# A two-layer graph kernel: the late tiles' exp moved from ScalarE to a power on GpSimd while the second layer's slots run

## Chip, cores, metric

The kernel runs on one core of a Trainium2 chip. The metric is the device time of one execution in microseconds, lower is better. Times below are the median of several runs and one profiled execution with its trace.

## What is computed

Two layers follow each other on 2708 rows of 256 values. Each is an attention over a 0/1 adjacency matrix and then a mixture of eight experts, of which every row takes two. Cut to what matters here, the second layer's expert part is:

```
xf     = layernorm(x)                            # [2708, 256]
probs  = softmax(xf @ gate_w + gate_b)           # [2708, 8]
top2_vals, top2_idx = top_k(probs, 2)
cw     = zeros([2708, 8]) with top2_vals put at top2_idx
out    = sum over e of cw[:, e] * (gelu(xf @ W1[e] + b1[e]) @ W2[e] + b2[e])
x      = x + out
```

The weight of a row's expert is its probability among all eight, so the softmax's denominator is a sum over eight exps. In the first layer the two weights are divided by their own sum, so there only two exps are needed.

## The kernel before

**Tiles and order.** The 2708 rows are 21 tiles of 128 and one of 20. The kernel runs `layer0_attention`, the first layer's experts, `layer1_attention`, the second layer's experts and a last sum. The second layer's attention handles its tiles in groups of 6, 6, 4, 3 and 3.

**Routing (`Experts.route`, L995 on).** Each tile, once its attention is done, is normalized and routed: its logits, the two best experts, the softmax weights, and the place of each row in the DRAM table `disp`, where the rows of one expert stand together. Two indirect DMAs from GpSimd (L1099) put the tile's rows there. `route` is a Python generator. A `Line` object holds the generators of the tiles in work and advances each of them by one `yield` per `line.step()`; a new tile is begun every `gap` steps. So the steps of several tiles are interleaved, and the program's order follows from the yields.

For the second layer (`own_norm` false) the steps of a tile are, in order: row statistics, with GpSimd raising the variance to the power -0.5 (L215); an empty step; the normalized row (L219) and the index copy on GpSimd (L1025); the row's copy (L1038), logits, best values, `p` = logit minus the best logit (L1065) and the one-hot masks; the exp of `p`, eight columns, with the sum of the row taken along by ScalarE (L1077); two small products on TensorE that count rows per expert (L1080, L1081); and last the division by the sum (L1084, L1085), the destination rows and the two scatters.

**Slots (`Experts.slots`).** The expert work is cut into slots of 128 rows of one expert. For a slot, `fetch_weights` (L1260, GpSimd's queue) brings the expert's weights into one of four buffers `ring`, unless they are there already, and `fetch_rows` (L1283, SyncE's queue) brings its rows; both are issued three slots ahead. Then TensorE transposes the rows (`tp`, copied by ScalarE to `xe`, L1326), multiplies with the first weights (`mm`, L1343), ScalarE applies Gelu (`hT`, L1351), TensorE multiplies with the second weights (`acc`, L1359, called the down product here), VectorE forms `y` (L1365), and GpSimd scatters `y` to the DRAM table `xd` (L1371). The down product of a slot runs inside the next slot. `slot(s)` calls `line.step()` twice, once before the fetches and the down product and once behind them, with `gap` 3 for the second layer. So the tiles that were not yet routed when the slots begin are routed between the slots, one new tile every one and a half slots.

The slots up to number 19 are laid out (`place`, L1114 on) when 14 tiles have been routed; the others when the last tile is done and the line is empty, at the latest in slot 17.

**What sets the order.** In the second layer's slots the program's order is kept on TensorE, ScalarE and VectorE (`manual_schedule`), and on SyncE throughout. GpSimd's queue is ordered by a planner that estimates when each instruction can start; so are all engines but SyncE in the first layer's slots. Every engine runs its queue in order. `y` has three buffers, the down product's `acc` two and `hT` two.

Of the kernel before, what the change touches and what calls it, by code (L numbers as in the profile page):

```python
# [2 lines left out]

# [6 lines left out]
F32 = mybir.dt.float32  # L10
# [5 lines left out]
AF = mybir.ActivationFunctionType  # L16
ALU = mybir.AluOpType
AX = mybir.AxisListType
PSUM = bass.MemoryType.PSUM

P = 128
# [3 lines left out]
E = 8  # L25
# [44 lines left out]
def adj_ffn_kernel(ctx: ExitStack, tc: tile.TileContext, a: dict, out: bass.AP):  # L70
    nc = tc.nc

    const = ctx.enter_context(tc.tile_pool(name="const", bufs=1))
# [24 lines left out]
        before, ones, pattern=[[1, P]], base=0, channel_multiplier=-1,  # L98
        compare_op=ALU.is_gt, fill=0.0,
    )  # L100

    once_twice = const.tile([P, 2, 2], F32, name="once_twice")
    for i, value in enumerate((1.0, 1.0 + EPS, EPS, EPS * EPS)):
# [171 lines left out]
    class Line:  # L275
# [3 lines left out]
        def __init__(self, gap):  # L279
            self.gap, self.waiting, self.running, self.since = gap, [], [], gap  # L280
# [649 lines left out]
    class Experts:  # L930
        def __init__(self, layer, hidden, packed_weights, w_gate, gate_bias, own_norm, xd, disp, early):
            self.hidden, self.packed_weights, self.own_norm = hidden, packed_weights, own_norm
            self.w_gate, self.gate_bias, self.xd, self.disp = w_gate, gate_bias, xd, disp

            self.seen = const.tile([P, E], BF16, name=f"seen{layer}")
            nc.vector.memset(self.seen, 0.0)
            self.routed, self.begun, self.pads = 0, False, []
            self.written = []
            self.groups = [f"written{layer}", f"late{layer}", f"apart{layer}", f"after{layer}"]
            self.early = early  # L940
            self.side = "right" if own_norm else "left"


            n = FULL_AFTER[early]

            size = -(-(SURE - n) // RING)
            runs = [(0, 0, n // RING, 1), (n, size - 1, size, -1)]
            self.number = const.tile([P, SLOTS, 2], F32, name=f"number{layer}")
            number_i = const.tile([P, SLOTS], I32, name=f"number_i{layer}")
            for s0, c0, size, step in runs:  # L950
                nc.gpsimd.iota(
                    number_i[:, s0 : s0 + size * RING], pattern=[[step, size], [size, RING]],
                    base=c0, channel_multiplier=0,
                )
            s0 = n + size * RING
            nc.gpsimd.iota(
                number_i[:, s0:], pattern=[[1, SLOTS - s0]], base=s0 - n, channel_multiplier=0
            )
            nc.vector.tensor_copy(self.number[:, :, 0], number_i)
            nc.vector.tensor_scalar(  # L960
                self.number[:, :, 1], self.number[:, :, 0], float(P), None, ALU.mult
            )
# [32 lines left out]
        def route(self, t, x, logits=None):  # L995


            own_norm, xd, disp, seen = self.own_norm, self.xd, self.disp, self.seen
            w_gate, gate_bias = self.w_gate, self.gate_bias
            r = ROWS[t]  # L1000
# [61 lines left out]
            k = 2 if own_norm else E  # L1062
            p = small.tile([P, E], F32, name="p")
            den = small.tile([P, 2], F32, name="den")
# [9 lines left out]
                nc.vector.memset(sel, 0.0)  # L1074
            nc.vector.tensor_add(sel[:r], hot[:r, 0], hot[:r, 1])
            yield
            nc.scalar.activation(p[:r, :k], p[:r, :k], AF.Exp, accum_out=den[:r, 0:1])  # L1077
            yield
            ps = misc.tile([P, GROUP, P], F32, name="misc").rearrange("p g n -> p (g n)")
            nc.tensor.matmul(ps[:, :E], before, sel, start=True, stop=False)  # L1080
# [207 lines left out]
            return xg  # L1288

        def run(self, line):  # L1290
            with (
                self.scope,
                tc.tile_pool(name="ffn2", bufs=2, side=self.side) as two,
                tc.tile_pool(name="ps_mm", bufs=2, space=PSUM) as ps_mm,
                tc.tile_pool(name="ps_tp", bufs=2, space=PSUM) as ps_tp,
                tc.tile_pool(name="ps_acc", bufs=2, space=PSUM) as ps_acc,
            ):
                with ExitStack() as order:
                    if not self.own_norm:

                        order.enter_context(tc.manual_schedule(engines={
                            mybir.EngineType.PE,
                            mybir.EngineType.Activation,
                            mybir.EngineType.DVE,
                        }))
                    self.slots(two, ps_mm, ps_tp, ps_acc, line)
# [239 lines left out]
```

## Time and profile before

| | us |
|---|---|
| median of 7 runs | 1275.02 (1268.92 to 1278.78) |
| profiled execution | 1278.89 |
| its span | 1277.1 |
| last attention product of the second layer's groups (L756) begins | 1034.71 |
| first product of the second layer's slot 0 (L1343) begins | 1039.12 |
| of slot 1 | 1043.82 |
| of slot 9 | 1089.35 |
| of slot 13 | 1110.73 |
| granted TensorE clock over the span | 0.979 |

Starts are counted from the span's start. The prediction and the text after it show lines of the profile. In a timeline a line has the start, the duration, the engine, the line of the kernel, the operation, the output and the inputs; in brackets stands how long the engine was idle before, and what ended that. In a list of groups a line has the shapes, the count, then busy time in total, the mean in ns, and the idle time before with its releasers. PE is TensorE, PEld its weight loads, DVE VectorE, ACT ScalarE, POOL GpSimd, SP SyncE.

### The profile page before, as it was taken

To read this page: it belongs to the slowest core of one execution; us is meant where nothing else is said; L and a number is where in the kernel's file an instruction comes from. 1 tells how busy PE (TensorE), PEld (TensorE's weight loads), DVE (VectorE), ACT (ScalarE), POOL (GpSimd) and SP (SyncE) were. 2 spreads that over 40 slices of the span, in tenths; PEclk is the share of its full clock that TensorE was granted. 3 is DMA by queue.
4 is the path that set the end of the run, shared out by engine and by line. 5 is a ranking of instruction groups with operands and counts; after the bars stand their busy time and mean duration, and the time that the engine had idled before them with its cause. 6 is when DMAs were issued, how large, how long until landed. Compare 5 with 4: busy or idle time off the path is not lost. (4 is left out here: it accounts for less than half of the span.)

```text
span 1277.1 us, 20738 instructions
## 1 busy us (share of the span) xinstructions
PE 1201.3 (94%) x7144; PEld 967.2 (76%) x7144; DVE 514.2 (40%) x1906; ACT 445.4 (35%) x1298; POOL 415.7 (33%) x519
## 2 busy tenths in 40 slices
PE   7999999999999999999999999999999977899990
PEld 4776666656656666689999999997999966799880
DVE  7613742733634526541121121115867763211114
ACT  3222222212211222442323323324777656344440
POOL 4100110111110213253333343335635556455450
PEclk9999999999999999999999999999999988999995
DMA  8601364997955905556557944543005125544458
GB/s 270 229 1 52 119 173 121 262 230 179 264 140 128 204 17 223 193 139 205 157 175 229 349 117 125 161 107 94 1 10 192 62 63 183 160 141 134 138 182 265
DMA packets 107239, 197.80 MB, mean 155 GB/s; under 512 B 26753, under 2 KB 81718, under 8 KB 100986
## 3 DMA queue, kind: packets, MB, share of 16 engines
q1 hardware_dynamic: 77276, 110.09, 30.6%
q0 software_dynamic: 27040, 83.56, 20.7%
q10 hardware_dynamic: 2814, 2.77, 0.7%
q8 instruction: 59, 0.97, 0.3%
q14 instruction: 50, 0.41, 0.1%
HBM read 263.63 MB, written 66.12 MB: 258 GB/s over the span
## 5 line engine op out<-in xcount | busy, mean ns | idle before, releaser
L1343 PE MATMUL mm<-xe,ring 128*128 128x128 f32 x2192 | 270.8, 281 | 19.2 <-ACT xe L1326 10.7
L1343 PEld LDWEIGHTS mm<-xe,ring 128*128 128x128 f32 x2192 | 259.6, 195 | 35.7 <-ACT xe L1326 14.0
L1359 PE MATMUL acc<-ring,hT 128*128 128x256 f32 x1096 | 261.9, 383 | 1.6 <-ACT hT L1351 1.1
L1351 ACT ACTIVATE hT<-mm,ring 128x128 f32<-128x128 f32 x548 | 156.4, 369 | 295.7 <-issue 181.5
L1359 PEld LDWEIGHTS acc<-ring,hT 128*128 128x128 f32 x1096 | 199.9, 192 | 24.2 <-ACT hT L1351 1.3
L508 PE MATMUL acc<-v,p 128*128 128x257 f32 (+1 forms) x880 | 208.9, 389 | 0.0
L451 PE MATMUL s<-g,xnT 128*128 128x512 f32 x420 | 205.1, 603 | 2.6 <-DVE mT L463 2.6
L1365 DVE SCALAR_TENSOR_TENSOR y<-acc,xg,bias 128x256 f32<-128x256 f32 x92 | 44.5, 484 | 402.9 <-PE acc L1359 388.1
L1260 POOL DMA_INDIRECT ring<-L_ffn_packed,weight_row x98 | 103.2, 1053 | 195.1 <-issue 88.8
L508 PEld LDWEIGHTS acc<-v,p 128*128 128x128 f32 (+1 forms) x880 | 153.0, 190 | 18.1 <-issue 0.8
L1099 POOL DMA_INDIRECT disp<-row,to x88 | 87.8, 997 | 179.3 <-DVE to L1096 83.1
L215 POOL TENSOR_TENSOR ln_rs<-ln_rs,minus_half 128x2 f32<-128x2 f32 x88 | 66.1, 753 | 192.3 <-DVE ln_rs L211 174.8
L750 PE MATMUL acc<-parts,m 128*128 128x266 f32 x924 | 127.6, 295 | 0.0
L463 DVE TENSOR_SCALAR mT<-s 128x512 fp8e4<-128x512 f32 x105 | 71.9, 687 | 132.0 <-ACT p L462 129.4
L750 PEld LDWEIGHTS acc<-parts,m 128*128 128x128 f32 x924 | 118.3, 187 | 4.4 <-ACT raw L777 0.9
L462 ACT ACTIVATE p<-s 128x512 f32<-128x512 f32 x105 | 62.1, 594 | 164.2 <-PE s L457 163.0
L451 PEld LDWEIGHTS s<-g,xnT 128*128 128x128 f32 x420 | 75.1, 191 | 49.0 <-issue 41.7
L1378 POOL DMA_INDIRECT xd<-y,xg x45 | 70.9, 1576 | 88.1 <-issue 35.5
L457 PEld LDWEIGHTS <-apart 128*128 128x128 fp8e4 x420 | 32.5, 98 | 60.5 <-issue 60.5
L720 ACT CAST m<-mT 128x512 fp32r<-128x512 fp8e4 (+4 forms) x168 | 71.6, 474 | 12.3 <-PE acc L750 7.6
L338 DVE TENSOR_SCALAR apart<-adj 128x677 fp8e4<-128x677 int32 x80 | 41.2, 516 | 55.2 <-DMA adj<-in_adj_dram 54.4
L1371 POOL DMA_INDIRECT xd<-y,xg x47 | 46.8, 995 | 21.1 <-PE tp L1316 8.9
(242 smaller groups left out, 1109.9 us busy)
## 6 DMA issues: line engine op xcount, KB each, us to landing
adj<-in_adj_dram SPq DMA_DIRECT2D x84, 338.5 KB
L_ffn_packed<-in_L_ffn_W_dram SPq DMA_DIRECT2D x16, 1024.0 KB
xg<-disp SPq DMA_DIRECT2D x98, 129.0 KB
L_ffn_packed<-in_L_ffn_W_dram SPq DMA_DIRECT2D x16, 512.0 KB
neighbours<-mT SPq DMA_DIRECT2D x5, 1408.0 KB
mT<-neighbours SPq DMA_DIRECT2D x5, 1408.0 KB
xin<-in_x_dram SPq DMA_DIRECT2D x42, 128.0 KB
ring<-L_ffn_packed SPq DMA_DIRECT2D x4, 1154.0 KB
```

The source lines that it names most:

```text
L215: nc.gpsimd.tensor_tensor(rs[:r, 1], rs[:r, 0], minus_half[:r], ALU.pow)
L451: nc.tensor.matmul(ps[:kr, :nb], xnT[:, c, k0 : k0 + kr], g[:, c, :nb], start=(c == 0), stop=False,)
L463: nc.vector.tensor_scalar(mT[:kr, k, :], ps[:kr, :nb], -BIG / 2, None, ALU.is_gt, saturate=False,)
L508: nc.tensor.matmul(accs[j][:r], p[keys, q0 : q0 + r], v[keys, k, :], start=(k == 0), stop=(k == NT - 1),)
L720: nc.scalar.copy(m[:, : q1 - q0], mTs[b][:, k, q0 - b * BN : q1 - b * BN])
L750: nc.tensor.matmul(acc[:r], masks[t], parts[:, k, i], start=(k == 0 and i == 0), stop=False,)
L1099: nc.gpsimd.indirect_dma_start(disp[:], bass.IndirectOffsetOnAxis(ap=to[:r, j : j + 1], axis=0), rows2[:r, j], None,)
L1260: start = nc.gpsimd.indirect_dma_start(w, None, packed[:], bass.IndirectOffsetOnAxis(ap=self.weight_row[:, s : s + 1], axis=0), bounds_che ...
L1343: nc.tensor.matmul(ps[:, i, :], w[:, c * hidden + f * P : c * hidden + (f + 1) * P], xe[:, c, :], start=(c == 0), stop=(c == DC - 1),)
L1351: nc.scalar.activation(hT[:, f, :], ps[:, i, :], AF.Gelu, bias=w[:, b1 + f : b1 + f + 1])
L1359: nc.tensor.matmul(ps, hT[:, f, :], w[:, w2 + f * D : w2 + (f + 1) * D], start=(f == 0), stop=(f == hc - 1),)
L1378: start = nc.gpsimd.indirect_dma_start(xd[:], at, y, None, bounds_check=N - 1, oob_is_err=False, compute_op=ALU.add)
```

## The change

A constant `euler`, 128 x 8 values of e, is written by GpSimd at the start. `Experts` gets a flag `running`, false until `run` is called. In `route`, the first layer, and the second layer's tiles that reach the exp before its slots run, keep ScalarE's exp with its running sum. A tile of the second layer that reaches it while the slots run takes e to the power of `p` on GpSimd instead, yields, and sums the eight columns on VectorE in the next step. Such a tile then has one step more than before; the products, the division and the scatters come in the steps behind.

```
+    euler = const.tile([P, E], F32, name="euler")
+    nc.gpsimd.memset(euler, math.e)
...
-            self.written = []
+            self.written, self.running = [], False
...
             yield
-            nc.scalar.activation(p[:r, :k], p[:r, :k], AF.Exp, accum_out=den[:r, 0:1])
+            if own_norm or not self.running:
+                nc.scalar.activation(p[:r, :k], p[:r, :k], AF.Exp, accum_out=den[:r, 0:1])
+            else:
+
+                nc.gpsimd.tensor_tensor(p[:r, :k], euler[:r, :k], p[:r, :k], ALU.pow)
+                yield
+                nc.vector.tensor_reduce(den[:r, 0:1], p[:r, :k], AX.X, ALU.add)
             yield
...
         def run(self, line):
+            self.running = True
```

More of the change, by code (lines that the diff above doesn't have):

```diff
@@ L2 @@
 from functools import partial
+import math
 import concourse.bass as bass
```

## The prediction, made before the changed kernel ran

> **What bounds the kernel now.** I read the page first, then all instructions of the line to be replaced (L1077), then ScalarE's and GpSimd's timelines from 1038 to 1110 us, the stage in which the second layer's slots run beside late tiles, and last the waits of that stage alone.
>
> Part 1 of the page (engine, busy us, share of the span, instructions):
>
> ```profile
> PE 1201.3 (94%) x7144; PEld 967.2 (76%) x7144; DVE 514.2 (40%) x1906; ACT 445.4 (35%) x1298; POOL 415.7 (33%) x519
> ```
>
> TensorE is busy for 94% of the span, so another engine's work counts only where TensorE waits for it. L1077, the exp:
>
> ```profile
> L1077 ACT ACTIVATE p<-p x44: 203/204/222, 149.8 to 1080.0; 128x2 f32<-128x2 f32 x21, 128x8 f32<-128x8 f32 x21, 20x2 f32<-20x2 f32 x1, 20x8 f32<-20x8 f32 x1
> L1077 ACT ACT_TABLE_LOAD  x7: 1283/1283/1283, 533.6 to 1078.8; - x7
> ```
>
> The exp itself is small, 204 ns. But 7 of the 44 come with a table load of 1283 ns: two in the first layer's slots (533.6 and 548.3), five in the second's. ScalarE's timeline shows one of the five (start, us, engine, line, operation):
>
> ```profile
> 1043.38 0.39 ACT L1326 COPY xe<-tp 128x256 f32<-128x256 f32 x1
> 1043.79 1.28 ACT L1077 ACT_TABLE_LOAD   x1
> 1045.08 0.21 ACT L1077 ACTIVATE p<-p 128x8 f32<-128x8 f32 x1
> 1045.19 0.19 ACT L1077 ACTIVATION_READ_ACCUMULATOR p<-p 128x1 f32 x1
> 1045.29 0.49 ACT L1336 ACTIVATE bias<-ring,xg 128x256 f32<-128x256 f32 x1
> 1045.80 1.28 ACT L1351 ACT_TABLE_LOAD   x1
> 1047.09 1.14 ACT L1351 ACTIVATE hT<-mm,ring 128x128 f32<-128x128 f32 x4
> ```
>
> One exp costs two loads, its own and the Gelu's behind it, and that Gelu (hT) and the next chunk's xe stand behind both. The other four are at 1052.12, 1057.61, 1067.16 and 1078.75. Who waits, from 1038 to 1110 (us in total, times, longest):
>
> ```profile
> PEld mm L1343 <- ACT xe L1326: 11.8, 6, 4.5
> PE mm L1343 <- ACT xe L1326: 9.7, 5, 4.1
> PE mm L1343 <- DMA ring<-L_ffn_packed,weight_row: 2.5, 1, 2.5
> ```
>
> TensorE's first product of a slot waits for xe. By mm's starts, slots 1 to 13 take from 1043.82 to 1110.73, 66.9 us; later slots have a pitch of 3.73, which would make 44.8. So 22 us are lost here. But GpSimd is full too:
>
> ```profile
> 1051.75 0.99 POOL L1099 DMA_INDIRECT disp<-row,to  x1 [0.30 <-issue]
> 1053.05 0.99 POOL L1099 DMA_INDIRECT disp<-row,to  x1 [0.30 <-issue]
> 1054.07 0.73 POOL L215 TENSOR_TENSOR ln_rs<-ln_rs,minus_half 128x2 f32<-128x2 f32 x1
> 1054.99 1.22 POOL L1260 DMA_INDIRECT ring<-L_ffn_packed,weight_row  x1 [0.19 <-issue]
> 1056.52 1.01 POOL L1371 DMA_INDIRECT xd<-y,xg  x1 [0.31 <-DVE lg L1054]
> ```
>
> It issues back to back from 1048.74 to 1075.1, the weight fetches (ring) in one queue with the tiles' row scatters (disp). The fetch for slot 6 goes out at 1061.34, lands 7.6 us later, and TensorE waits the 2.5 us above for it.
>
> **The change, part by part.** *Removed:* five exp (0.2 and 0.19 each) and ten table loads, 10 x 1.283 = 12.8 us of ScalarE. What reaches TensorE, by its waits: 0.60 at 1048.55 and 1.23 at 1057.65, 0.75 at 1062.53 (put to issue, but xe was 0.06 old), and of the 4.09 at 1078.79 the 1.28 of the load at 1076.03; 3.9 in all. The rest of the 12.8 lies beside products. The wait at 1078.79 also slows what follows: by the table of stretches the granted clock is 0.58 from 1080 to 1085 (1.00 from 1085 to 1090), mm takes 3.78 instead of 2.05 and the down product 2.60 instead of 1.89, 2.4 more. What is late next: of the first three waits (2.6), whatever gets to slot 6 sooner meets the weights; only what their fetch gains goes through.
>
> *Added on GpSimd:* one power of 128x8 per tile, five in all. No row shows its duration. The nearest rows (busy, mean ns):
>
> ```profile
> L215 POOL TENSOR_TENSOR ln_rs<-ln_rs,minus_half 128x2 f32<-128x2 f32 x84 | 63.3, 755 | 188.2 <-DVE ln_rs L211 170.7 <-DVE ln_mv L210 6.5 <-DVE z L252 5.3
> L663 POOL TENSOR_TENSOR kept<-kept,L_gnn_b_fc_b 128x256 f32<-128x256 f32 x21 | 15.9, 756 | 0.0
> L1025 POOL COPY row<-token 128x2 int32<-128x2 int32 x21 | 4.3, 203 | 7.8 <-DVE row L219 4.1 <-DVE den L1084 3.7
> ```
>
> Two columns of power take 755, as long as 256 columns of addition. Lower end: columns cost nothing, 0.76. Upper end: everything scales with them, 4 x 0.755 = 3.0. If the 0.2 of a copy is fixed and the rest scales: 0.2 + 4 x 0.55 = 2.4. The same operation (L215) is the nearest row and its shape differs by 6 columns only; I take 1.5 with the gap behind it, nearer to the lower end. The constant euler is a memset of 128x8 before the first load (such a memset takes 110): 0.1 under the input's loading.
>
> *Moved:* what follows the exp comes one line step later, and there are two steps per slot. Counting steps from slot 0's first, the five exp stand at 1, 4, 7, 10, 13 and the scatters at 3, 6, 9, 12, 15; these become 4, 7, 10, 13, 16. The routing of the remaining slots (place) stays in slot 8: step 15 was the second of slot 7, 16 is the first of slot 8, just ahead of it. Two scatters more fall behind the fetch for slot 6, and two behind that for slot 9, with their 2.6 us.
>
> *The queue as a sum.* From 1048.74 to the fetch for slot 13, GpSimd issues 9 fetches (1.4 each with the gap), 9 result scatters (1.3), 10 row scatters (1.3), 3 ln_rs (0.9) and 3 index copies (0.4): 41.2 us, so with no wait that fetch could go out at 1089.9. It goes out at 1103.08, so the queue had 13.2 to spare. The first power falls into an idle stretch (1042.8 to 1048.7); four at 1.5 take 6.0. So by GpSimd 7.2 can be won, and the fetch for slot 13 is one that TensorE waits for now (landing 7.5 later, wait of 0.96 at 1110.73). The fetch for slot 6 is ready at 1048.74 + 2 x 1.4 + 2 x 1.3 + 2.6 + 2 x 0.9 + 0.4 + 1.5 = 1060.4, 0.9 before its present time.
>
> *Added on VectorE:* five sums of 128x8, like L1096 (169): 0.8 in all beside products. The sum is a new wait: it stands ahead of y in VectorE's queue and waits for a power that may lie behind two scatters. y then is late, its result scatter with it, and behind that the next fetch. The second and third tile meet this at about 1 us each by the queue; I charge 1.2 in all, between nothing and 4 (1 per tile in the full stretch).
>
> *Sum.* By the queue 7.2 - 1.2 = 6.0. By TensorE: 0.9 through slot 6, 1.28 and 2.4 at slot 7: 4.6. I take **5.5**. The profiled execution took 1278.89 us (span 1277.1, 1.8 around it), so 1273.4 there; the median of the runs is 1275.02, 3.9 lower, and 5.5 below it is **1269.5**.
>
> *The Trainium skill here.* "ScalarE: Activation LUTs", section "What ACT_TABLE_LOAD costs", gives 1283 ns for the load, as the rows do, and 1380 more of drain, 2.66 for a switch; by it the ten switches would be 26.6. The rows show 10 ns between the load's end and the Gelu at 1047.09, so 12.8 holds. "GPSIMD Engine Reference", section "Engine selection", speaks against the change: it gives elementwise work to VectorE and counts GpSimd as about half as fast. Its 2.6 cycles per element (section 3.1) would make six more columns an estimated 13 ns, and the gain by the queue some 9; but that is an addition's price, and L215 shows that a power's is another.
>
> **The rivals.** *More, 9 to 11 us, 1264 to 1266.* ScalarE and VectorE also stand still from 1071.5 to 1076.0 and from 1093.2 to 1095.2 for a reason that I can't read. If that hangs on the late Gelu, 4.5 goes with it: 4.6 + 4.5 = 9.1, and the queue allows 13.2 - 4 x 0.95 = 9.4 at a power of 0.76. For it: VectorE's y at 1076.13 is released together with the Gelu's table load. Against: no table load stands near 1095. 0.15.
>
> *No change, within 3.8 us.* Weights and y keep TensorE waiting as before, with a power of 2.4: 13.2 - 10 = 3.2, less 1.2 for VectorE, gives 2, or 1273. It holds also if the exp isn't in the stage where TensorE waits, that is, if the change takes away nothing that counts. Against that: the five loads stand between slots 0 and 7. 0.31.
>
> *Slower.* GpSimd becomes the bound. The place is its queue between the fetches for slots 4 and 13: if power plus VectorE's wait come to more than 13.2 over four tiles, 3.3 each, the fetch for slot 13 goes out later than now. At 3.0 and 1 per tile that is 16, 2.8 too much, and each fetch that lands late brings the slow clock, 2.4: 5.2 slower, 1280. The same sign has a new order on GpSimd or in the first layer's slots, which the planner sets and which a further instruction may shift. 0.14.
>
> **How the numbers follow.** Forecast (4 to 9 faster): 0.40. About 0.3%, 3.8 us, is what a measurement of this kernel tells from no change. Faster is forecast and the first rival, 0.55; same 0.31; slower 0.14. The range takes in the first rival and the last one up to its price of 5.2: 1264 to 1280; a dearer power, a new order of the whole or a gain beyond 11, less than 2 in 10 together, lie outside.
>
> **What would show it.** Right: no table load in the second layer's slots but the one at their start; xe no longer ahead of mm's waits; fetches for slots 10 to 13 some 6 us earlier; a power of 1 to 2 us. Wrong: a power over 3 us; VectorE's sum waiting over 2 us for GpSimd, with y behind it; or mm of slots 6 to 9 waiting longer for weights than now; or first-layer slots that moved.

## The result: about 0.5% slower, and the profile after

| | before | after |
|---|---|---|
| median, us | 1275.88 (35 runs) | 1281.63 (14 runs) |
| profiled execution, us | 1278.89 | 1280.44 |
| its span, us | 1277.1 | 1278.6 |

The ratio of after to before is 1.0051 with an interval of 1.0033 to 1.0069: 6.5 us slower (4.2 to 8.8). The forecast was 5.5 us faster, and 1281.63 lies outside the range of 1264 to 1280.

The engines' busy time, part 1 of the page of after:

```profile
PE 1200.8 (94%) x7144; PEld 967.3 (76%) x7144; DVE 514.9 (40%) x1911; ACT 431.1 (34%) x1278; POOL 423.4 (33%) x525
```

ScalarE has lost 14.3 us of work (445.4 before) and GpSimd gained 7.7 (415.7). So the change did what it says. All uses of the two lines in the trace of after (engine, operation, shortest/median/longest ns, first and last start):

```profile
L1084 POOL TENSOR_TENSOR p<-euler,p x5: 1631/1669/1689, 1044.7 to 1087.4; 128x8 f32<-128x8 f32 x4, 20x8 f32<-20x8 f32 x1
L1081 ACT ACT_TABLE_LOAD  x2: 1283/1283/1283, 536.1 to 550.9; - x2
```

The exp's five loads in the second layer's slots are gone, and the power takes 1.67 us. Who waits from 1036 to 1115 us in after (us in total, times, longest):

```profile
DVE den L1086 <- POOL p L1084: 24.1, 5, 9.1
PE misc L1129 <- DVE seen L1099: 5.2, 1, 5.2
PE misc L1090 <- DVE seen L1099: 3.2, 2, 1.9
PE mm L1353 <- ACT xe L1336: 4.0, 4, 1.2
PE mm L1353 <- DMA ring<-L_ffn_packed,weight_row: 3.2, 4, 1.8
```

The wait of mm for xe has fallen from 9.7 to 4.0. In its place stands a new chain: VectorE's sum waits 24.1 us for the power, `seen` (the running count of rows per expert, L1099) comes late, and TensorE waits 8.4 us for it, 5.2 of that at `place` (L1129). GpSimd's queue of after ahead of the last tile's power shows why:

```profile
1077.12 1.10 POOL L1269 DMA_INDIRECT ring<-L_ffn_packed,weight_row  x1 [0.18 <-issue]
1078.52 1.01 POOL L1108 DMA_INDIRECT disp<-row,to  x1 [0.30 <-issue]
1079.83 0.98 POOL L1108 DMA_INDIRECT disp<-row,to  x1 [0.30 <-issue]
1081.11 1.00 POOL L1381 DMA_INDIRECT xd<-y,xg  x1 [0.30 <-issue]
1082.11 0.21 POOL L1028 COPY row<-token 20x2 int32<-20x2 int32 x1
1082.47 1.06 POOL L1269 DMA_INDIRECT ring<-L_ffn_packed,weight_row  x1 [0.16 <-issue]
1083.84 1.01 POOL L1381 DMA_INDIRECT xd<-y,xg  x1 [0.30 <-issue]
1085.16 0.97 POOL L1108 DMA_INDIRECT disp<-row,to  x1 [0.30 <-issue]
1086.44 0.98 POOL L1108 DMA_INDIRECT disp<-row,to  x1 [0.30 <-issue]
1087.44 1.69 POOL L1084 TENSOR_TENSOR p<-euler,p 20x8 f32<-20x8 f32 x1
```

Back to back: the power's input is ready at 1078.47 (VectorE's L1068), but four row scatters, two result scatters, a fetch and a copy stand ahead of it, 9 us. VectorE and TensorE of after at the same place:

```profile
1089.16 0.15 DVE L1086 TENSOR_REDUCE den<-p 20x1 f32<-20x8 f32 x1 [9.09 <-POOL p L1084]
1089.34 0.48 DVE L1375 SCALAR_TENSOR_TENSOR y<-acc,xg,bias 128x256 f32<-128x256 f32 x1
...
1090.13 0.24 DVE L1099 TENSOR_TENSOR seen<-seen,sel 128x8 bf16<-128x8 bf16 x1
```

```profile
1090.46 0.17 PE L1129 MATMUL misc<-seen,ones 128*128 128x8 bf16 x1 [5.24 <-DVE seen L1099]
1090.49 3.43 PE L1369 MATMUL acc<-ring,hT 128*128 128x256 f32 x8
```

VectorE runs nothing for 9.09 us; y, the division and `seen` all stand behind the sum. TensorE idles for 5.24 us, and the down product after it takes 3.43 instead of 1.89 us.

These profiles show the wait, but not the loss. From the first Gelu of slot 0 to that of slot 15, before takes 78.0 us and after 75.8, so after is 2.2 us shorter where the change acts. Its span is 1.5 longer since slot 0 comes 2.7 later and the rest takes 1.0 more; 2.5 of the 2.7 are there at the first table load of the first layer's slots (533.6 and 536.1), which in the second pair below stands at 534.1 and 534.4.

**A second pair of profiles.** Two single executions can't show what the change is worth, since runs of one kernel spread over 1269 to 1285 us. So both kernels were profiled once more, on another chip, on which the kernel before is faster (median 1268.81 of 17).

> The kernel before once more, unchanged, for a second profile of it, since single executions differ by some 3 us. Both theories: time within 1269 to 1282 us. If GpSimd's stretch from the slot-5 weight fetch to the last scatter had slack by chance in the first profile, its gaps of 1.75 and 7.03 us will be elsewhere or gone; if they belong to the kernel, one of 5 us or more is there again.

> The changed kernel once more, unchanged, for a second profile of it. Both theories: the time within 1277 to 1289 us. Theory of the queue and the wait together: GpSimd's stretch from the slot-5 weight fetch to the last scatter is without a gap above 1.5 us again and 42 to 44 us long, VectorE's wait for p is over 20 us in sum, and TensorE waits over 4 us for the count at the place.

("Slot-5 weight fetch" in these expectations is a slip: the fetch meant is the first of the full stretch, which the prediction counts as slot 4's.) Measured: 1267.61 and 1276.41, 8.8 apart and each about 1 us under its expected range. From the first Gelu of slot 0 to that of slot 15 these two take 65.6 and 75.1 us, 9.5 apart, so the whole difference lies in these slots. Nearly all of it lies in one: counted from slot 0, after is 1.2 us behind at slot 8 and 9.8 at slot 9. There stand the count for `place` and a down product, first before, then after:

```profile
1080.50 0.17 PE L1120 MATMUL misc<-seen,ones 128*128 128x8 bf16 x1
1080.53 1.98 PE L1359 MATMUL acc<-ring,hT 128*128 128x256 f32 x8
```

```profile
1088.32 0.17 PE L1129 MATMUL misc<-seen,ones 128*128 128x8 bf16 x1 [6.89 <-DVE seen L1099]
1088.35 3.52 PE L1369 MATMUL acc<-ring,hT 128*128 128x256 f32 x8
```

GpSimd's queue in the first profile of before had a hole:

```profile
1078.23 1.00 POOL L1371 DMA_INDIRECT xd<-y,xg  x1 [0.31 <-issue]
1086.26 1.04 POOL L1260 DMA_INDIRECT ring<-L_ffn_packed,weight_row  x1 [7.03 <-ACT bias L1336]
```

In the second profile of before there is none:

```profile
1077.70 1.00 POOL L1371 DMA_INDIRECT xd<-y,xg  x1 [0.31 <-issue]
1079.01 1.04 POOL L1260 DMA_INDIRECT ring<-L_ffn_packed,weight_row  x1 [0.30 <-DVE hot L1091]
1080.36 0.99 POOL L1371 DMA_INDIRECT xd<-y,xg  x1 [0.31 <-issue]
```

So not every execution of the kernel has the hole. It comes behind the standstill that the prediction could not read. It isn't one accident either: at the same fetch, that for slot 10, two kernels without a power on GpSimd show holes of 5.88 (`no_loads`) and 3.20 us (`only_step`, both below), on a chip with a median of 1274.7 for before. The stretch from 1080 to 1095 us in the second pair, first before, then after (window, its length, then busy us of PE, PEld, DVE, ACT, POOL, granted clock, DMA share, GB/s):

```profile
1080.00:1095.00 15.00, 13.70 (x93) 12.51 (x92) 6.60 (x26) 6.83 (x23) 9.52 (x11) 1.00 0.64 192
```

```profile
1080.00:1095.00 15.00, 8.11 (x46) 7.13 (x46) 6.77 (x31) 3.06 (x11) 11.13 (x12) 0.77 0.33 99
```

TensorE has 93 products on record in these 15 us before, and 46 after at a clock of 0.77; GpSimd is the one engine that is clearly busier. The wait of VectorE is 24.1 us again.

### The profile page after: what moved, and what is told of

Its sections match the earlier page's. It is cut to its first block, busy times and chain, and to the rows that moved or that the text cites. A ratio compares the mean times of both kernels' runs of the same rounds, so it can differ in the third digit from the quotient of the medians.

```text
span 1278.6 us, 20728 instructions
## 1 busy us (share of the span) xinstructions
PE 1200.8 (94%) x7144; PEld 967.3 (76%) x7144; DVE 514.9 (40%) x1911; ACT 431.1 (34%) x1278; POOL 423.4 (33%) x525
```

## The experiments

Three theories. **Wait**: VectorE's in-order wait for the power holds `seen` and y. **Queue**: GpSimd's time itself paces the slots, whoever waits. **Step**: the later step. Every ratio is to the kernel before on the same chip, with its interval; us are that ratio times the median of before there (1267.8 to 1268.9 for `only_two`, `pow_no_loads` and all kernels without the weights' bytes, 1274.7 or 1274.8 for the others).

### What the loads and the step are worth

`no_loads`: the late tiles' exp becomes a copy with a sum, so nothing is loaded (the experts' weights are wrong); nothing is added.

```
-            nc.scalar.activation(p[:r, :k], p[:r, :k], AF.Exp, accum_out=den[:r, 0:1])
+            late = self.running and not own_norm
+            nc.scalar.activation(p[:r, :k], p[:r, :k], AF.Identity if late else AF.Exp, accum_out=...)
```

> The kernel before, but ScalarE's exp of the five late tiles is an identity with the same running sum, so the ten table loads are gone and nothing is added (the expert weights are then wrong; the routing and all work stay the same). If the loads are worth what the prediction says (4.6 us by TensorE's waits, up to 9 by the queue), it is 4 to 9 us faster than the kernel before. If the loads lie beside other work and only the first rival's stalls count, it is within 2 us of the kernel before.

1.0007 (0.9984 to 1.0029), 0.9 us. The 12.8 us of loads were hidden, as far as this interval tells. The same hole stands in GpSimd's queue as in the first profile of before, so the loads don't cause it:

```profile
1078.72 1.00 POOL L1375 DMA_INDIRECT xd<-y,xg  x1 [0.31 <-issue]
1085.61 1.04 POOL L1263 DMA_INDIRECT ring<-L_ffn_packed,weight_row  x1 [5.88 <-issue]
```

Taking the power to another place could therefore not bring much either: this kernel does the late tiles' exp for nothing, and is no faster.

`only_step`: the kernel before with one empty `yield` for late tiles.

> The kernel before with exp on ScalarE, and only one empty step more behind it for the five late tiles. Theory 3, the later step itself makes it slower since the last count now stands just ahead of the layout of the remaining slots: 3 us or more slower than the kernel before. Theories 1 and 2: within 2 us of it.

1.0008 (0.9988 to 1.0028), 1.0 us: the step theory falls, which expected 3 or more.

### The power alone, and in doses

`only_pow`: the kernel before, loads and exp in place, and a power into a tile that nobody reads.

```
+            if self.running and not own_norm:
+                spare = small.tile([P, E], F32, name="spare")
+                nc.gpsimd.tensor_tensor(spare[:r, :k], euler[:r, :k], best[:r, :k], ALU.pow)
```

> The kernel before, exponential, table loads and line steps as they were, with one more GpSimd instruction per late tile at the place of the exponential: e to the eight best logits, into a tile that nothing reads. It adds five times some 1.65 us to GpSimd's queue, four of them between the weight fetches of the slots, and no wait of VectorE. Theory of the queue (GpSimd's time between the fetches paces the stage): about 4 us slower than before (2 to 7). Theory of the in-order wait (VectorE's sum behind the power holds seen and y): within 2 us of before, since nobody waits for the tile.

1.0040 (1.0017 to 1.0063), 5.1 us. Nobody waits for this power, and it costs nearly as much as the whole change. The cost is seen in the runs and not in its one profile, whose span (1276.4) is no longer than the first one of before; GpSimd's queue there still has gaps of 2.0 and 5.8 us ahead of the fetches for slots 12 and 13. `only_two` has that last line twice; `pow_no_loads` has it once, with the loads taken away as in `no_loads`.

> The kernel before with two powers per late tile on GpSimd into a tile that nothing reads, 3.3 us per tile in all, loads and exponential in place, no wait added. If GpSimd's time goes through, twice the loss of one such power, 8 to 12 us slower than before; if the changed kernel's loss comes through VectorE's wait and the single power's 5 us were something else, 3 to 6 us slower as the single power is.

> The kernel before with the power on GpSimd into a tile that nothing reads, as in the earlier experiment, and the exponential turned into a copy with a sum, so that no table is loaded (the experts' weights are wrong); no step is added and nothing waits for the power. It is the changed kernel without the wait of VectorE and without the later step. Theory of the queue, loads hidden: 3 to 6 us slower than before, like the power alone with the loads in place. If the loads were worth something beside it, 3 us or more under that kernel, so within 2 us of before.

`only_two` 1.0107 (1.0072 to 1.0142), 13.6 us, above the 8 to 12 of the queue theory; `pow_no_loads` 1.0059 (1.0035 to 1.0083), 7.5 us, above the 3 to 6; both intervals reach into the expected ranges. Both ran where the kernel before is faster; with less idle time there, more of a longer queue goes through, which is a reading and was not tried by itself.

`double_pow`: the changed kernel with a second power of exponent one behind the first. `cheap`: the changed kernel with `ALU.add` for `ALU.pow`.

> The changed kernel with a second power behind the first on GpSimd, p to the power of one, so the values stay the same. It adds another five times some 1.65 us to GpSimd's queue and to the wait of VectorE's sum. Theory of the queue: each power between the fetches goes through, so 4 to 7 us slower than the changed kernel, 10 to 13 over before. Theory of the in-order wait: the wait grows by 1.65 us in each tile, but it is felt only where TensorE waits for the count, at two or three places, so 2 to 4 us slower than the changed kernel.

> The changed kernel with an addition in the power's place (the weights of the experts come out wrong, the routing is the same). The instruction stays on GpSimd at its place in the queue, and VectorE's sum still waits for it a step later, but it takes some 0.2 us and not 1.65. Theory of the queue: back to within 2 us of before, so some 4 us under the changed kernel. Theory of the in-order wait: the wait of VectorE for p stays over 15 us in sum, since the instruction stands behind the same scatters and fetches, and the time stays 3 us or more above before.

`double_pow` 1.0088 (1.0053 to 1.0123), 11.2 us, as the queue theory had it. VectorE's wait is 33.1 there and TensorE's at `place` 9.1. `cheap` 1.0022 (1.0001 to 1.0044), 2.8 us: between the theories. Its instruction takes 0.21 us but stands behind the same scatters and fetches:

```profile
DVE den L1086 <- issue: 10.1, 2, 7.1
DVE den L1086 <- POOL p L1084: 6.5, 2, 5.1
PE misc L1129 <- DVE seen L1099: 0.5, 1, 0.5
```

The two waits put to "issue" are waits for the addition as well, since the sum starts 0.03 us behind its end; the longer one:

```profile
1080.81 0.22 POOL L1084 TENSOR_TENSOR p<-euler,p 20x8 f32<-20x8 f32 x1
1081.06 0.15 DVE L1086 TENSOR_REDUCE den<-p 20x1 f32<-20x8 f32 x1 [7.08 <-issue]
```

So the sum waits 16.6 us here, over the 15 that the wait theory expected, against 24.1 in the changed kernel and 33.1 with two powers. The longer the queue, the longer this wait; most of it comes from the scatters and fetches that stand ahead, not from the power. TensorE's wait at `place` has shrunk from 5.2 to 0.5.

### Moving the wait

`free_sum`: the sum reads `euler` and doesn't wait (the experts' weights are wrong). `early_pow`: the power one step earlier, sum and division last. `sum_last`: the power at the exp's step, no step added, sum and division behind all else that VectorE does for the tile.

```
+            if late:
+                nc.vector.tensor_reduce(den[:r, 0:1], p[:r, :k], AX.X, ALU.add)
+                nc.vector.reciprocal(den[:r, 1:2], den[:r, 0:1])
+                nc.vector.tensor_scalar(rows2[...], p[:r, :2].unsqueeze(2), den[:r, 1:2], None, ALU.mult)
```

> The changed kernel, but VectorE's sum reads the constant euler and not the power's result, so it waits for nothing; the power stays, and only the division one step later still waits for it (weights wrong). Theory 1, VectorE stands in its queue for the power behind GpSimd's scatters and holds back the count that TensorE needs: 3 us or more below the changed kernel. Theory 2, the power's 1.65 us in GpSimd's full queue delays the weights: within 2 us of the changed kernel, some 6 us slower than before.

> The power is issued one step earlier, with the subtraction that feeds it, and the sum and the division come last in the last step, behind the rows' destinations and the running count; no step is added, so scatters and counts stand where they stood before. Theory 1: VectorE hardly waits, the loads' gain comes through, 3 to 7 us faster than the kernel before. Theory 2 (GpSimd's time): still as slow as the changed kernel, 4 to 7 us slower than before. Theory 3 (the added step): as without it, near the kernel before or faster.

> The power on GpSimd at the exponential's own step with no step added, and the sum, the reciprocal and the division moved behind everything else that VectorE does for the tile, so that the running count and the place come before the wait. Table loads gone as in the changed kernel. Theory of the queue: GpSimd has the same powers to do, so 3 to 7 us slower than before, as the changed kernel is. Theory of the in-order wait: the wait no longer stands ahead of the running count, so within 2 us of before or faster, and TensorE's waits for the count are gone.

Measured 1.0034 (1.0014 to 1.0053), 1.0041 (1.0015 to 1.0068) and 1.0018 (0.9993 to 1.0043): 4.3, 5.2 and 2.3 us. The first and the last lie between the two theories, the second where the queue theory had it. In `free_sum` the division, which reads p as well, took the wait over; in `early_pow` the tile's ln_rs, also on GpSimd, did (5.4 in the first profile of before):

```profile
DVE row L1094 <- POOL p L1084: 11.5, 4, 5.5
PE misc L1129 <- DVE seen L1099: 4.8, 1, 4.8
```

```profile
DVE row L222 <- POOL ln_rs L218: 16.5, 5, 5.2
```

Both `early_pow` and `sum_last` take TensorE's wait for `seen` away. Of the two only `sum_last` leaves VectorE without so long a wait in its place (9.6 for ln_rs, 5.9 for the power). It is the best form of the idea, and still no better than the kernel before; its interval doesn't part it from before, nor clearly from the changed kernel.

### Without the weights' bytes

In these the second layer's fetches are issued but move nothing (all rows out of bounds), so every slot uses the first experts' weights. Cut to the second layer's case:

```
-                self.weight_row[:, s0:s1], same[:, s0:s1], float(FAR), weights, op0=ALU.mult, op1=ALU.add,
+                self.weight_row[:, s0:s1], weights, float(FAR), weights, op0=ALU.add, op1=ALU.max,
```

> The kernel before, in which the weight fetches of the second layer's slots are still issued at their places by GpSimd but move no data (all rows out of bounds), so every slot uses the first experts' weights and the output is not the reference's; the routing and the number of slots stay. Exponential and table loads are as in the kernel before. If the bytes of the real fetches hold TensorE (slots 5 to 7, 12 and 13), faster by 4 to 12 us; if the place of the fetches in GpSimd's queue paces the stage and not their bytes, within 2 us of before. It is the base for the next two kernels.

> The same without weight data, and with the late tiles' exponential turned into a copy with a sum, so that no table is loaded in the slots (the experts' weights in the rows are wrong too). Against the kernel without weight data alone: if the bytes of the weights had hidden the loads, 3 to 9 us faster; if GpSimd's queue hides them, within 2 us.

> The changed kernel without weight data (the slots use the first experts' weights). Against the kernel before without weight data: theory of the queue, in the form that a power only costs by making a real weight fetch later, within 2 us; theory of the queue in the form that scatters and fetches of every kind pace the slots, 4 to 7 us slower; theory of the in-order wait, 4 to 7 us slower too, with the wait of VectorE for p still over 15 us.

> The kernel before without weight data (the slots use the first experts' weights), exponential and table loads in place, with the power on GpSimd into a tile that nothing reads. Against the kernel without weight data, which took 0.9935 of before: if GpSimd's full queue alone makes the loss, 7 us slower or more, so about level with before; if the loss of 12 us in the changed kernel without weight data comes through VectorE's wait for the power, within 3 us of that base, so 0.992 to 0.996 of before.

> The changed kernel without weight data, with an addition of some 0.2 us in the power's place (the experts' weights are wrong as well). The wait of VectorE and the added step stay, GpSimd's queue is shorter by four times 1.45 us. If GpSimd's time alone makes the loss, back to the base without weight data, 0.990 to 0.996 of before; if the wait at its place in the queue makes it, 1.000 of before or more, as the changed kernel without weight data; if both, between them.

> The power at the exponential's step and the sum behind everything else that VectorE does for the tile, as in the earlier kernel, without weight data (the slots use the first experts' weights). GpSimd has the same powers as the changed kernel without weight data, which took 1.0026 of before; only the wait no longer stands ahead of the running count. If the queue alone makes that loss, 1.000 or more; if the wait ahead of the count makes the larger part, 0.994 to 0.998, as the power that nobody waits for (0.9968).

| without weight data | ratio to before | against the first row, us | GpSimd's full stretch, us |
|---|---|---|---|
| kernel before | 0.9935 (0.9912 to 0.9958) | | 34.0 |
| and no loads | 0.9923 (0.9900 to 0.9946) | -1.5 | 34.1 |
| and a power that nobody waits for | 0.9968 (0.9948 to 0.9989) | +4.2 | 40.3 |
| addition for power, with the wait | 0.9964 (0.9939 to 0.9988) | +3.7 | 36.9 |
| power, sum last | 0.9967 (0.9949 to 0.9985) | +4.1 | 40.5 |
| the whole change | 1.0026 (1.0000 to 1.0053) | +11.5 | 42.8 |

The full stretch goes from the fetch for slot 4 to the end of the last tile's last scatter. In the kernel without weight data it has no gap above 0.6 us and takes 34.0, as in the second profile of before (34.0, gaps up to 0.3 beside the one of 0.56 behind the first fetch); in the first profile of before, holes included, it takes 42.45. Four powers of 1.66 make 40.6 of it; measured 40.3, and 40.3 in `only_pow`, with the weights in place; 46.9 with two powers (`only_two`). The rest up to 42.8 (42.8 in both profiles of after as well) are three gaps of 0.70, 0.70 and 1.31 in the changed kernel without weight data; the profile puts the last two to VectorE and names no releaser for the first.

Without the bytes the kernel before is 8.2 us faster (5.3 to 11.2), so they do hold TensorE; by the profiles mostly behind these slots (slot 0 to 15 in 63.5 us against 65.6, the rest in 152.4 against 156.9). With this cover gone the loads still bring only 1.5 us, and the two intervals overlap: that speaks for GpSimd's queue as what hides them, not the weights' bytes. The change costs 11.5 us here, above the 4 to 7 of either theory; the queue without the wait 4.2; the wait behind a short instruction 3.7; and with the full power but the sum behind `seen`, 4.1 again. By the intervals in the table each of these differences is uncertain by some 4 us. So the 3.7 alone isn't clear of zero, and the 4.2 just is. Clear are the two steps down from the whole change: without the wait it costs 7.3 us less, with a short instruction 7.8 less. So both theories hold. Whether together they cost more than 4.2 and 3.7 is not settled, since a plain sum lies within the uncertainty. As read from the traces, the long queue makes the power late, and the in-order wait hands that lateness to `seen`, y and TensorE. The waits without weight data, of the whole change and then with the addition:

```profile
DVE den L1086 <- POOL p L1084: 23.9, 5, 8.9
PE misc L1129 <- DVE seen L1099: 5.4, 1, 5.4
```

```profile
DVE den L1086 <- POOL p L1084: 16.3, 4, 6.9
PE misc L1129 <- DVE seen L1099: 2.9, 1, 2.9
```

## Why the prediction was wrong, step by step

*Removed loads (3.9 of waits and 2.4 of slow clock).* Wrong. Taking all of them away moved the time by +0.9 us (between 2.0 faster and 3.7 slower). Rightly said was that the early waits only go through as far as the weights let them: by the Gelu's starts, after is ahead of before by 3.3 us at slot 4 in the second pair. But it is the fetch for slot 5 that takes this back, and the prediction left it out: the second power stands ahead of it, it goes out 8.4 us behind that for slot 4 instead of 6.2, and TensorE waits for it.

```profile
1063.90 3.50 PE L1353 MATMUL mm<-xe,ring 128*128 128x128 f32 x16 [2.07 <-DMA ring<-L_ffn_packed,weight_row]
```

At slot 5 after is 2.6 us behind, at slot 6 0.2 ahead. The fetch for slot 6, forecast 0.9 sooner, goes out 12.6 us behind that for slot 4 in all four profiles. The 1.28 and 2.4 at slot 7 were read beside a standstill of that execution; in the second profile of before, with the loads in place, TensorE waits 0.88 us for slot 7's xe instead of 4.09, and its product takes 2.05 instead of 3.78.

*Power, 1.5 us.* Right in kind, 1.67; the lower of the sensible values, and the upper end of 3.0 was idle.

*Moved step.* Right: no cost by itself that can be told (1.0 us in `only_step`, between 1.5 faster and 3.6 slower).

*The queue, "13.2 to spare".* **This is the first step that failed.** The sum of 41.2 us was right: the second profile of before goes from the fetch for slot 4 to that for slot 13 in 41.0. There, nothing is to spare. The prediction compared the sum with one execution (54.3), in which the queue stood for 1.74, 7.03 and 4.73 us, and took these standstills for time that powers can fill. In after the stretch is 52.3 and 51.0. Gaps stand in the traces of `no_loads` and `only_step` too, on a chip with the slower median. But they can't be counted on as slack: on another such chip `only_pow` costs 5.1 us over its runs, though its profile has gaps as well. Why the powers don't vanish in them there, no trace shows.

*VectorE's wait, 1.2 us.* **The second.** Its wait came to 24.1 us, TensorE's behind it to 8.4. The prediction named y behind the sum, but not `seen`, which stands there too, nor the last tile: its count is what `place` needs, and its power lies behind eight other instructions. The upper end of 4 was therefore far too low as well. What this wait costs in time is measured only without the weights' bytes: 7.3 us of the 11.5.

*The rivals.* "More" falls: the standstill is there without any load (`no_loads`), and gone with all loads in place (second profile of before). "Slower" was the right mechanism at the right place: power and wait came to 1.67 and 4.8 per tile (24.1 over five), above its point of 3.3. Its sign, a later fetch for slot 13, shows in the second pair (51.0 us behind the fetch for slot 4 instead of 41.0), not in the first. Its 5.2 us are near the 6.5 measured, but by luck: it put 3.0 for the power and 1 for the wait, where 1.67 and 4.8 were measured. It got 0.14 because its condition was held against slack that wasn't there. "A new order" on GpSimd was not tried by itself; `only_pow` gives no sign of it, as its full stretch is that of before and four powers.

*The Trainium skill.* "GPSIMD Engine Reference", section "Engine selection", spoke against the change, and its sign came out so. What was measured is another reason, though: the price of the power and the queue that it stands in; no run puts this work on VectorE. The estimate of 13 ns for six more columns from its section 3.1 doesn't hold for a power: 1.67 - 0.755 = 0.91 us.

**Still open:** what holds the signal in the standstill. In the first profile of before, the product of slot 6 ends at 1071.5 by its record, and the engines that wait for it go on at 1076; nothing in the trace is shown to be the cause. Ahead of it that product waits 2.49 us for its weights and begins 7.7 us after their fetch; in the second profile it is 1.48 and 6.4. From 1070 to 1074 us the granted clock is 0.63 and 0.52 in the first, 1.00 in the second. This goes with the standstill and is not shown to make it. Open too is why the same kernel takes 1274.7 on one chip and 1268.8 on another; whether that is this standstill, one profile on the faster chip doesn't settle.

## What to carry to other kernels

Add up a queue's own instructions first. Don't take its gaps in a single profile for slack: here they were nearly gone in a second profile, and a kernel whose profile had some still paid 5 us for its powers. Before work goes to a full in-order queue, ask where in that queue its input becomes ready and what lies ahead of it; and of the engine that then waits, list all that stands behind the wait, above all the values that others count on (here a running count that TensorE needs). A load that shows a wait right behind it can still be worth nothing that can be measured: here 12.8 us of loads were.

## What the runs showed of the hardware

- A GpSimd power of f32 takes 0.755 us for 128x2 and 1.67 for 128x8, so by these two points an estimated 0.15 per column and 0.45 beside; 20 rows take as long as 128 (1.69), and exponent one as long as the exps' (1.67 in `double_pow`). An addition of 128x8 takes 0.21.
- An indirect DMA costs GpSimd about 1.0 us and 0.3 up to the next one, also when it moves no data: 34.0 us for the same stretch with and without the weights' bytes.
- The table load took 1283 ns each time, with the next ACTIVATE 10 ns behind it.
- After TensorE's waits of 5.24 and 6.89 us at `place` the next eight products took 3.43 and 3.52 us, instead of 1.98 without a wait; the granted clock from 1080 to 1095 us was 0.77 in the second profile of after, 1.00 in that of before.
